# Two layers on one core: the last two weight tiles of the memory layer stay in SBUF and open its second pass

## The chip, the cores and the metric

The kernel runs on one core of one Trainium2 chip. The metric is the device time of one execution, in microseconds; the median of several executions is compared. Beside the timed executions there is one that the hardware profiler recorded. It is a separate execution with a time of its own, and all durations of single instructions come from it.

## The reference

Two layers over x of shape (2, 512, 64, 64), that is 2 images of 4096 positions with 512 channels. Both normalise their input by groups of channels and add their result to x. Layer 0 is a Mamba block (projections, a short convolution, a selective scan over 4096 positions with 1024 inner channels of 16 states); the change does not touch it. Layer 1 is a memory of 1024 rows m:

```python
def _L1_conv_ref(x, m):
    xf = jnp.transpose(x, (0, 2, 3, 1)).reshape(-1, c)   # 8192 positions x 512
    xn = _l2norm(xf)
    mn = _l2norm(m)                                      # 1024 x 512
    score = xn @ mn.T
    idx = jnp.argmax(score, axis=1)
    counts = jax.ops.segment_sum(jnp.ones(xf.shape[0], dtype=xf.dtype), idx, num_segments=k)
    esum = jax.ops.segment_sum(xf, idx, num_segments=k)
    emean = esum / (counts[:, None] + EPS_MEAN)
    new_m = m * MOVING_AVG_RATE + emean * (1.0 - MOVING_AVG_RATE)
    soft = jax.nn.softmax(score, axis=1)
    out = soft @ new_m
...
x = x + _L0_conv_ref(_gn(x), ...)
x = x + _L1_conv_ref(_gn(x), L1_conv_m)
```

new_m depends on every position, since any of them may have chosen any row. So out can't begin before all scores are known, and layer 1 has two passes.

## The kernel before

Everything is in float32. Layer 0 works in a hand-written order: its instructions go through a wrapper (line 36 in the profile) that stamps them with their place, and a table of due times sets when each step is issued. It writes x + layer 0 to DRAM as `x1d`, 256 KB at a time (tile `xo`).

Layer 1 (from line 1025) cuts the 2 x 4096 positions into 16 tiles of TT = 512, `tiles[0]` to `tiles[15]`, and each tile into SUB = 4 sub-tiles of 128 positions. P is 128, KB = 8 blocks of memory rows, CB = 4 blocks of channels. There is no order by hand here: within each engine's queue the framework's scheduler places the instructions[...]. A pool of tiles (`tc.tile_pool`) hands out `bufs` buffers for each tag, and a pool that is opened after others were closed uses their memory again; an instruction that writes into such memory waits until the last reader of what lay there is done.

*Pass 1* (loop from L1138). For each sub-tile, PE multiplies the normalised x (`xf`, loaded from `x1d` at L1060, scaled at L1062) with the normalised memory rows, which lie in `win`: the scores `pc` (L1148), 128 positions by 1024 rows. ACT copies them to `sc` (L1160) and takes the exponential `ex` (L1163), DVE scales it by the sum (L1168) and finds the largest score and its index `ix` (L1173, L1175), and `fx` is that index as a float (L1177).

Then two side branches run behind the scores:

- `match` and `add_rows` (L1098 to L1120), one sub-tile late. Positions of a sub-tile that chose the same row are added up on PE (`dg`, `pr`, `sel`, `pe`); POOL gathers the chosen rows from a table in DRAM (L1113), DVE adds, POOL scatters them back (L1120). There are two tables, `tabs[0]` and `tabs[1]`, for even and odd sub-tiles, so that a gather needn't wait for the scatter just before it.
- `exT_part` (L1088), DEFER = 6 sub-tiles late. Pass 2 needs the exponentials with the memory rows on the partitions. PE transposes 128 x 128 blocks of `ex` into `px` (L1093), four blocks to a PSUM bank, and ACT copies the bank into `exT` (L1094). A sub-tile has two such halves. When all four sub-tiles of a tile are in, ACT's queue stores `exT` (2 MB) to DRAM as `exd` (L1135). When the scores end, seven sub-tiles, 14 halves, are still to be transposed.

Between the scores of one sub-tile, `turn` (L1070) transposes the next tile's x through one PSUM bank, tag `pt`. [...]

*Pass 2* (from L1195). `new_m(kb)` loads rows kb of both tables into `e0` and `e1` (L1205, SP's queue), and DVE adds them, divides by the count, and adds the result to the decayed memory row in `win` (L1206 to L1213); `mrow` is the code's name of that part of `win`. Then PE multiplies `exT` with it: `po` (L1231), 8 products for each of the 4 channel blocks of a tile; in the trace each product is two records. Tiles go in pairs (FIRST = 2). For the first pair the blocks of memory rows are the outer loop, so that PE can start as soon as block 0 is ready:

```python
if k0 == 0:
    for kb in range(KB):
        new_m(kb)
        for j in range(len(some)):
            for cb in range(CB):
                mm(j, cb, kb)
```

For each tile SP loads `exT` from `exd` (L1223) and `xt` from `x1d` (L1225), DVE adds `po` to `xt` (L1248), and SP stores it to the output (L1249, 1 MB).

The pool `p3` (xt, and exT of every second pair) exists from before pass 1. The pool `pr3` (exT of the other pairs, e0, e1, rc) is opened after pass 1's pools are closed and lies on their memory. Pass 1's own exT buffers, two, are in `p2`.

Of the kernel before, what the change touches and what calls it, by code (L numbers as in the profile page):

```python
# [8 lines left out]
F32 = mybir.dt.float32  # L9
# [9 lines left out]
P = 128  # L19
# [30 lines left out]
def kernel(  # L50
# [17 lines left out]
    nc = tc.nc  # L68
    B, C, L = x.shape
# [6 lines left out]
    KB = K // P  # L76
# [6 lines left out]
    TT = 512  # L83
    NT = L // TT
    SUB = TT // P
# [48 lines left out]
    ROW = C + 16  # L134
# [5 lines left out]
    ov = out.rearrange("b (cb p) t -> b p cb t", p=P)  # L140
# [45 lines left out]
    with ExitStack() as l0:  # L186
        nc = InOrder(tc, tc.nc)
# [837 lines left out]
    nc = tc.nc  # L1025
    exd = [[dram.tile([P, KB, TT], F32, name=f"exd{b}_{t}") for t in range(NT)] for b in range(B)]
    p3 = ctx.enter_context(tc.tile_pool(name="q3", bufs=2))
    DEFER = 6
    KH = K // TT
    KBH = KB // KH  # L1030
    tiles = [(b, t) for b in range(B) for t in range(NT)]
# [11 lines left out]
    with ExitStack() as s:  # L1043
        p1 = s.enter_context(tc.tile_pool(name="p1", bufs=1))
        p2 = s.enter_context(tc.tile_pool(name="p2", bufs=2))
        p_ex = s.enter_context(tc.tile_pool(name="p_ex", bufs=DEFER + 1))
        ps_t = s.enter_context(tc.tile_pool(name="ps_t", bufs=1, space=PSUM))
        ps_s = s.enter_context(tc.tile_pool(name="ps_s", bufs=2, space=PSUM))
        ps_x = s.enter_context(tc.tile_pool(name="ps_x", bufs=1, space=PSUM))
# [6 lines left out]
        def load_xf(k):  # L1056

            b, t = tiles[k]
            xf = p2.tile([P, CB, TT], F32, tag="xf", name="xf")
            nc.sync.dma_start(xf, x1d[b][:, :, t * TT : (t + 1) * TT])  # L1060
            for cb in range(CB):
                nc.vector.tensor_scalar(  # L1062
                    xf[:, cb], xf[:, cb], gmu[1][b][:, cb : cb + 1], grs[1][b][:, cb : cb + 1],
                    ALU.subtract, ALU.mult,
                )
            xT = p2.tile([P, SUB, C], F32, tag="xT", name="xT")
            ss = p2.tile([P, SUB], F32, tag="ss", name="ss")
            return xf, xT, ss
# [16 lines left out]
            inv_norm(r, cur[2], wk)  # L1085
            return r

        def exT_part(ex, exT, i, kh):  # L1088

            px = ps_x.tile([P, KBH, P], F32, tag="px", name="px")  # L1090
            for q in range(KBH):
                kb = kh * KBH + q
                nc.tensor.transpose(px[:, q], ex[:, kb * P : (kb + 1) * P], ident)  # L1093
            nc.scalar.copy(  # L1094
                exT[:, kh * KBH : (kh + 1) * KBH, i * P : (i + 1) * P], px
            )
# [27 lines left out]
        behind = None  # L1124
        late = []

        def transpose_late(kh):
            if late:
                ex, exT, i, k = late[0]
                exT_part(ex, exT, i, kh)  # L1130
                if kh == KH - 1:
                    late.pop(0)
                    if i == SUB - 1:
                        b, t = tiles[k]
                        nc.scalar.dma_start(exd[b][t], exT)  # L1135

        for k in range(len(tiles)):
            cur, r = nxt, r_next  # L1138
            xf, xT, _ = cur
            if k + 1 < len(tiles):  # L1140
                nxt = load_xf(k + 1)
            exT = p2.tile([P, KB, TT], F32, tag="exT", name="exT")
            for i in range(SUB):
                pc = ps_s.tile([P, K], F32, tag="pc", name="pc")
                for kh in range(KH):
                    cols = slice(kh * TT, (kh + 1) * TT)
                    for cb in range(CB):
                        nc.tensor.matmul(  # L1148
                            pc[:, cols], xf[:, cb, i * P : (i + 1) * P], mn[:, cb, cols],
                            start=cb == 0, stop=cb == CB - 1,  # L1150
                        )
                    if kh == KH - 1 and behind is not None:
                        sel = match(*behind)
                    if k * SUB + i + DEFER < len(tiles) * SUB:
                        transpose_late(kh)
                if behind is not None:
                    add_rows(*behind, sel)

                sc = p2.tile([P, K], F32, tag="sc", name="sc")
                nc.scalar.copy(sc, pc)  # L1160
                ex = p_ex.tile([P, K], F32, tag="ex", name="ex")
                den = p2.tile([P, 1], F32, tag="den", name="den")
                nc.scalar.activation(ex, pc, AF.Exp, scale=r[:, i : i + 1], accum_out=den)  # L1163
                end = k == len(tiles) - 1 and i == SUB - 1

                def scale():
                    nc.vector.reciprocal(den, den)  # L1167
                    nc.vector.tensor_scalar_mul(ex, ex, den)  # L1168

                if not end:  # L1170
                    scale()
                mx = p2.tile([P, 8], F32, tag="mx", name="mx")
                nc.vector.max(mx, sc)  # L1173
                ix = p2.tile([P, 8], U32, tag="ix", name="ix")
                nc.vector.max_index(ix, mx, sc)  # L1175
                fx = p2.tile([P, 1], F32, tag="fx", name="fx")
                nc.vector.tensor_copy(fx, ix[:, 0:1])  # L1177
                if end:
                    scale()
                behind = k * SUB + i, xT, i, fx, ix  # L1180
                late.append((ex, exT, i, k))
                if k + 1 < len(tiles):
                    turn(nxt, i)
            if k + 1 < len(tiles):
                r_next = lengths(nxt)
        for kh in range(2 * KH):
            transpose_late(kh % KH)
        sel = match(*behind)
        for kh in range(KH):
            transpose_late(kh)  # L1190
        add_rows(*behind, sel)
        while late:
            for kh in range(KH):
                transpose_late(kh)

    with ExitStack() as s:
        pr3 = s.enter_context(tc.tile_pool(name="r3", bufs=2))
        ps_o = s.enter_context(tc.tile_pool(name="qo", bufs=8, space=PSUM))

        def new_m(kb):  # L1200

            e = []
            for i, tab in enumerate(tabs):
                e.append(pr3.tile([P, ROW], F32, tag=f"e{i}", name=f"e{i}"))
                nc.sync.dma_start(e[i], tab[kb * P : (kb + 1) * P])  # L1205
            nc.vector.tensor_add(e[0][:, : C + 1], e[0][:, : C + 1], e[1][:, : C + 1])  # L1206
            rc = pr3.tile([P, 1], F32, tag="rc", name="rc")
            nc.vector.tensor_scalar(rc, e[0][:, C : C + 1], 1.0, 1e-6, ALU.mult, ALU.add)
            nc.vector.reciprocal(rc, rc)
            nc.vector.tensor_scalar(  # L1210
                e[0][:, :C], e[0][:, :C], rc, 1.0 - RATE, ALU.mult, ALU.mult
            )
            nc.vector.tensor_add(mrow[:, kb], mrow[:, kb], e[0][:, :C])  # L1213


        FIRST = 2
        for k0 in range(0, len(tiles), FIRST):
            some = tiles[k0 : k0 + FIRST]
            pool = (p3, pr3)[k0 // FIRST % 2]
            ld, pos = [], {}  # L1220
            for b, t in some:
                exT = pool.tile([P, KB, TT], F32, tag="exT", name="exT1")
                nc.sync.dma_start(exT, exd[b][t])  # L1223
                xt = p3.tile([P, CB, TT], F32, tag="xt", name="xt1")
                nc.sync.dma_start(xt, x1d[b][:, :, t * TT : (t + 1) * TT])  # L1225
                ld.append((exT, xt))

            def mm(j, cb, kb):
                if kb == 0:
                    pos[j, cb] = ps_o.tile([P, TT], F32, tag="po", name="po1")  # L1230
                nc.tensor.matmul(  # L1231
                    pos[j, cb], mrow[:, kb, cb * P : (cb + 1) * P], ld[j][0][:, kb],
                    start=kb == 0, stop=kb == KB - 1,
# [8 lines that stand above are left out]
            for j, (b, t) in enumerate(some):  # L1242
                xt = ld[j][1]
                for cb in range(CB):
                    if k0 > 0:
                        for kb in range(KB):
                            mm(j, cb, kb)
                    nc.vector.tensor_add(xt[:, cb], xt[:, cb], pos.pop((j, cb)))  # L1248
                nc.sync.dma_start(ov[b, :, :, t * TT : (t + 1) * TT], xt)  # L1249


# [43 lines left out]
```

## Time and profile before

| | us |
|---|---|
| three timed runs | 5016.26, 5016.58, 5024.3; median 5016.58 |
| the profiled execution, its own time | 5005.66 |
| its span, first to last instruction | 5003.9 |
| layer 0 ends, first product of pass 1 | 3935.2 |
| last product of pass 1's scores done | about 4520.5 |
| last copy into exT done | 4542.5 |
| first product of pass 2 | 4555.41 |
| last add of pass 2 done | 4998.8 |

The mean granted clock of TensorE over the span is 0.968 of full speed.

Busy time, share of the span and number of instructions of each engine, from the page:

```profile
PE 4509.2 (90%) x22640; PEld 3483.1 (70%) x22640; DVE 4011.0 (80%) x3340; ACT 3529.2 (71%) x8885; POOL 3873.3 (77%) x2890
```

Layer 0 takes almost four fifths of the time, and most of the busy time of DVE, ACT and POOL is there. Layer 1 is PE's: of the 1068.7 us from 3935.2 on, 585 are pass 1 and 443 are the products of pass 2. Its two largest groups are these (busy us, mean ns of one | idle time just before them and what ended it):

```profile
L1231 PE MATMUL po<-exT,win 128*128 128x512 f32 x1024 | 442.7, 595 | 13.5 <-DVE win L1213 13.5
L1148 PE MATMUL pc<-win,xf 128*128 128x512 f32 x960 | 433.8, 592 | 0.0
```

Matmuls overlap, so the mean of one (595 ns) is more than its share of the time (0.43 us). In such rows the idle time is the engine's, and the name behind the arrow is the instruction that ended it.

The transfers of layer 1, with their size and the median from issue to landing:

```profile
exd<-exT ACTq DMA_DIRECT2D x16, 2048.0 KB, 6.3
exT<-exd SPq DMA_DIRECT2D x16, 2048.0 KB, 9.5
```

A row load e<-tab is 264 KB and lands after 2.9 us in the median (2.5 to 5.2), a load of xt or xf is 1 MB (5.8 to 6.0 us), a store of a tile's output 1 MB (10.7 us in the median where it shares the engines with a load).

### The profile page before, as it was taken

The page shows a single profiled execution, that of the slowest core. Times are in us where ns is not written, and L with a number is a line of the kernel's source. Part 1 is how long each engine was busy: PE and PEld are TensorE (multiplying, and loading weights), DVE is VectorE, ACT ScalarE, POOL GpSimd, SP SyncE. Part 2 cuts the span into 40 slices and gives each one's busy share as a digit, 9 for nine tenths or more (in the row PEclk, how much of TensorE's full clock was granted, in tenths as well). Part 3 has the DMA queues.
Part 4 walks back from the last instruction along what each step waited for, and adds up shares of the span by engine and source line. Part 5 has one row for each costly group of instructions (what it writes and reads, how often), then busy time and mean ns, then how long its engine had stood idle before and what let it go on. Part 6 is the DMA issues. An engine that isn't in the chain of part 4 may idle for free. (4 is left out here: it accounts for less than half of the span.)

```text
span 5003.9 us, 64865 instructions
## 1 busy us (share of the span) xinstructions
PE 4509.2 (90%) x22640; PEld 3483.1 (70%) x22640; DVE 4011.0 (80%) x3340; ACT 3529.2 (71%) x8885; POOL 3873.3 (77%) x2890
## 2 busy tenths in 40 slices
PE   6989889888889898998898989998886899998999
PEld 5777777777777777777777777777775555553444
DVE  5799999999999999999999999999998755553100
ACT  3788888888888888888888888888886455441000
POOL 4899999999999999999999999999999322220000
PEclk8999999999999999999999999999997899998999
DMA  5132122122222222222211212111212344334452
GB/s 214 46 108 64 64 68 67 68 67 68 71 68 68 68 68 68 75 81 77 76 64 64 66 66 70 64 64 64 66 60 106 111 162 149 137 135 165 159 164 84
DMA packets 175551, 447.72 MB, mean 89 GB/s; under 512 B 23384, under 2 KB 77784, under 8 KB 171000
## 3 DMA queue, kind: packets, MB, share of 16 engines
q1 hardware_dynamic: 162680, 375.41, 22.5%
q0 software_dynamic: 10240, 34.61, 2.2%
q10 hardware_dynamic: 2304, 33.56, 1.6%
q8 instruction: 179, 2.93, 0.2%
q14 instruction: 148, 1.21, 0.1%
HBM read 351.63 MB, written 91.88 MB: 89 GB/s over the span
## 5 line engine op out<-in xcount | busy, mean ns | idle before, releaser
L36 POOL TENSOR_TENSOR bu<-B,du 128x1020 f32<-128x1020 f32 (+1 forms) x1152 | 2453.5, 2146 | 29.0 <-DVE dA L36 15.6
L36 ACT ACTIVATE dA<-delta,A 128x256 f32<-128x256 f32 x4096 | 1957.6, 478 | 151.3 <-DVE hc L36 37.8
L36 DVE TENSOR_TENSOR_SCAN dA<-dA,bu 128x1024 f32<-128x1024 f32 x832 | 1904.3, 2289 | 61.9 <-ACT dA L36 57.0
L36 PE MATMUL yT<-ident,hc 128*128 128x128 f32 x8192 | 1095.9, 283 | 215.6 <-DVE hc L36 144.3
L36 PEld LDWEIGHTS yT<-ident,hc 128*128 128x128 f32 x8192 | 965.3, 145 | 326.9 <-DVE hc L36 198.8
L36 DVE TENSOR_TENSOR hc<-dA,C 128x1024 f32<-128x1024 f32 x832 | 1019.3, 1225 | 126.0 <-PE yT L36 40.7
L36 PE MATMUL pz<-x,win 128*128 128x256 f32 x4096 | 940.7, 383 | 15.7 <-POOL x L36 14.9
L36 PEld LDWEIGHTS pz<-x,win 128*128 128x128 f32 x4096 | 767.0, 192 | 117.2 <-POOL x L36 18.7
L36 PE MATMUL cv<-xi,cd 128*128 128x256 f32 x2048 | 468.9, 381 | 27.0 <-POOL xi L36 24.5
L36 PE MATMUL po<-z,wo 128*128 128x256 f32 x2048 | 477.2, 387 | 0.8 <-DVE z L36 0.8
L36 DVE TENSOR_TENSOR_SCAN h<-dA,bu 128x1024 f32<-128x1024 f32 x192 | 438.2, 2282 | 43.2 <-POOL hc L36 34.3
L1231 PE MATMUL po<-exT,win 128*128 128x512 f32 x1024 | 442.7, 595 | 13.5 <-DVE win L1213 13.5
L36 POOL TENSOR_TENSOR hc<-h,C 128x1024 f32<-128x1024 f32 x192 | 454.5, 2367 | 0.0
L36 PEld LDWEIGHTS cv<-xi,cd 128*128 128x128 f32 x2048 | 380.2, 191 | 84.6 <-POOL xi L36 31.2
L1148 PE MATMUL pc<-win,xf 128*128 128x512 f32 x960 | 433.8, 592 | 0.0
L36 PEld LDWEIGHTS po<-z,wo 128*128 128x128 f32 x2048 | 390.3, 195 | 54.5 <-DVE z L36 1.0
L1231 PEld LDWEIGHTS po<-exT,win 128*128 128x128 f32 x1024 | 195.6, 191 | 260.2 <-issue 260.0
L1248 DVE TENSOR_TENSOR xt<-xt,po 128x512 f32<-128x512 f32 x64 | 44.0, 689 | 375.2 <-PE po L1231 360.9
L36 ACT COPY carry<-dA 128x4 f32<-128x4 f32 x780 | 125.7, 161 | 310.5 <-DVE hc L36 304.7
L1148 PEld LDWEIGHTS pc<-win,xf 128*128 128x128 f32 x960 | 173.5, 190 | 175.9 <-issue 175.9
L1120 POOL DMA_INDIRECT tab<-rows,ix x64 | 63.2, 987 | 294.4 <-DVE den L1167 274.8
L36 PE MATMUL py<-ident,ys 128*128 128x128 f32 x512 | 84.7, 290 | 165.2 <-DVE q L36 100.2
(171 smaller groups left out, 5057.9 us busy)
## 6 DMA issues: line engine op xcount, KB each, us to landing
B<-bcd SPq DMA_DIRECT2D x128, 512.0 KB, 3.9
C<-bcd SPq DMA_DIRECT2D x128, 512.0 KB, 4.7
wo<-in_out_wT_dram SPq DMA_DIRECT2D x128, 512.0 KB, 5.2
exd<-exT ACTq DMA_DIRECT2D x16, 2048.0 KB, 6.3
exT<-exd SPq DMA_DIRECT2D x16, 2048.0 KB, 9.5
xl<-in_x_dram SPq DMA_DIRECT2D x32, 512.0 KB, 10.7
x<-in_x_dram SPq DMA_DIRECT2D x32, 512.0 KB, 3.7
xo<-in_x_dram SPq DMA_DIRECT2D x64, 256.0 KB, 4.9
```

The source lines that it names most:

```text
L36: ins = call(*args, **kwargs)
L1120: nc.gpsimd.indirect_dma_start(tab, at, rows, None)
L1148: nc.tensor.matmul(pc[:, cols], xf[:, cb, i * P : (i + 1) * P], mn[:, cb, cols], start=cb == 0, stop=cb == CB - 1,)
L1231: nc.tensor.matmul(pos[j, cb], mrow[:, kb, cb * P : (cb + 1) * P], ld[j][0][:, kb], start=kb == 0, stop=kb == KB - 1,)
L1248: nc.vector.tensor_add(xt[:, cb], xt[:, cb], pos.pop((j, cb)))
```

## The change

Four edits, all in layer 1:

- Pass 1's exT buffers move from `p2` to `p3` and are remembered in `kept`. The last FIRST = 2 tiles are not stored to `exd`. Pass 2's order becomes tiles 14, 15, 0, 1, ..., 13, and its first pair uses the kept buffers instead of loading them.
- The table rows e0 and e1 get buffers in `p3`, which no tile of pass 1 uses.
- In the last 14 halves, the transposes use `px` and the bank of `pt` in turn.
- The last tile's output is stored in four pieces of 256 KB, each after its own add.

```diff
+    kept = {}
+    FIRST = 2
...
-        def exT_part(ex, exT, i, kh):
+        def exT_part(ex, exT, i, kh, alt=False):
 
-            px = ps_x.tile([P, KBH, P], F32, tag="px", name="px")
+            if alt:
+                px = ps_t.tile([P, C], F32, tag="pt", name="px2")
+                px = px.rearrange("p (q k) -> p q k", k=P)
+            else:
+                px = ps_x.tile([P, KBH, P], F32, tag="px", name="px")
...
-        def transpose_late(kh):
+        def transpose_late(kh, alt=False):
             if late:
                 ex, exT, i, k = late[0]
-                exT_part(ex, exT, i, kh)
+                exT_part(ex, exT, i, kh, alt)
                 if kh == KH - 1:
                     late.pop(0)
-                    if i == SUB - 1:
+                    if i == SUB - 1 and k < len(tiles) - FIRST:
                         b, t = tiles[k]
                         nc.scalar.dma_start(exd[b][t], exT)
...
-            exT = p2.tile([P, KB, TT], F32, tag="exT", name="exT")
+            exT = p3.tile([P, KB, TT], F32, tag="exT", name="exT")
+            kept[tiles[k]] = exT
...
         for kh in range(2 * KH):
-            transpose_late(kh % KH)
+            transpose_late(kh % KH, kh % 2 == 1)
         sel = match(*behind)
         for kh in range(KH):
-            transpose_late(kh)
+            transpose_late(kh, kh % 2 == 1)
         add_rows(*behind, sel)
         while late:
             for kh in range(KH):
-                transpose_late(kh)
+                transpose_late(kh, kh % 2 == 1)
...
-                e.append(pr3.tile([P, ROW], F32, tag=f"e{i}", name=f"e{i}"))
+                e.append(p3.tile([P, ROW], F32, tag=f"e{i}", name=f"e{i}"))
...
-        FIRST = 2
-        for k0 in range(0, len(tiles), FIRST):
-            some = tiles[k0 : k0 + FIRST]
+        order = tiles[-FIRST:] + tiles[:-FIRST]
+        for k0 in range(0, len(order), FIRST):
+            some = order[k0 : k0 + FIRST]
...
-                exT = pool.tile([P, KB, TT], F32, tag="exT", name="exT1")
-                nc.sync.dma_start(exT, exd[b][t])
+                if k0 == 0:
+                    exT = kept[b, t]
+                else:
+                    exT = pool.tile([P, KB, TT], F32, tag="exT", name="exT1")
+                    nc.sync.dma_start(exT, exd[b][t])
...
-                nc.sync.dma_start(ov[b, :, :, t * TT : (t + 1) * TT], xt)
+                    if k0 + j == len(order) - 1:
+                        nc.sync.dma_start(ov[b, :, cb, t * TT : (t + 1) * TT], xt[:, cb])
+                if k0 + j < len(order) - 1:
+                    nc.sync.dma_start(ov[b, :, :, t * TT : (t + 1) * TT], xt)
```

## The prediction

> **What bounds the kernel now.** I read the chain of waits first, in order of time, to see which engine sets the end of each stage of layer 1, then the waits of PE and of SP's queue, then the timeline around the seam of the two passes. Columns of the chain: start, length, what.
>
> ```profile
> 4538.98 1.13 PE px L1093 x4
> 4540.77 1.13 PE px L1093 x4
> 4542.54 6.26 DMA exd<-exT
> 4549.57 3.05 DMA e<-tab
> 4555.41 442.70 PE po L1231 x1024
> ```
>
> Ahead of these lines the chain is PE's products of pass 1 (pc, L1148); behind them are 442.7 us of pass 2 without a gap. So both passes are bound by PE, and only the seam is not: last transposes, then the store of the last exT, then the load of table rows, then the first product of pass 2. PE's own waits from 3935 to 4556 (waited for: total, times, longest) agree:
>
> ```profile
> PE po L1231 <- DVE win L1213: 13.5, 1, 13.5
> PE px L1093 <- ACT exT L1094: 8.1, 12, 1.1
> PE gs_pm L36 <- DVE gs_w L36: 1.1, 1, 1.1
> ```
>
> 13.5 us idle before pass 2, 8.1 us in the last transposes, nothing else. What holds the table rows is in SP's waits:
>
> ```profile
> SPq L1205 <- DMA tab<-rows,ix: 83.2, 1, 83.2
> SPq L1205 <- DMA exd<-exT: 11.9, 1, 11.9
> ```
>
> SP waited for the last scatter into the table until about 4536.8 (the last load of pass 1 was issued at 4453.6, plus 83.2), and then 11.9 us more for the store of tile 15's exT, because the row buffers lie on memory that the store still reads. First row load: 4549.19. And the scatter itself was late (timeline):
>
> ```profile
> 4529.81 0.33 ACTq L1135 DMA_DIRECT2D exd<-exT  x1
> 4529.83 0.42 PEld L1093 LDWEIGHTS px<-ident,ex 128*128 128x128 f32 x4 [0.91 <-ACT exT L1094]
> 4529.83 0.65 PE L1093 MATMUL px<-ident,ex 128*128 128x128 f32 x4 [0.68 <-ACT exT L1094]
> 4529.90 0.98 POOL L1120 DMA_INDIRECT tab<-rows,ix  x1 [3.60 <-DVE rows L1119]
> ```
>
> It was issued together with the 2 MB store of tile 14's exT; in half-microsecond windows the DMA engines then run at up to 524 GB/s until 4536.5. The scatter before it (POOL, 4523.66) had the engines to itself: its traffic, 253 and 287 GB/s, lies in 4525.0 to 4526.0, ending 1.4 us after POOL was done with it.
>
> **The change, part by part.**
>
> *No store of tiles 14 and 15, row buffers of their own.* Both holds go. Chain of the last sub-tile, from the rows above: its gather, pe, and the DVE adds are not touched (the built order moves dg behind two more exT copies, to about 4525.3 from 4524.87, but the gather is what ends last before the add, at 4528.87). POOL issues the last scatter at 4529.90 to 4530.88, traffic ends 1.4 us later, 4532.3, seen by SP at about 4532.7 (bounds 4532.3 and 4534.0). The rows of table 0, whose last scatter was done by 4527, are in by then: in the built order SP issues both loads of table 0 first, then both of table 1. So one load decides, issued at 4532.8. The page gives 2.9 us median from issue to landing (2.5 to 5.2); before, the first add began 3.75 us after the first of four loads. I take 3.2: add at 4536.0 (bounds 4535.0 and 4538.2). DVE then interleaves two row blocks in the built order; ahead of the end of the first lie two adds 0.70, two rc 0.15, two reciprocals 0.16, one scaling 0.49 and one add into win 0.69, with eight steps of some 0.04 between: 3.5 us where one block alone took 2.35. With 0.15 us to PE (win done 4555.26, product 4555.41): first product 4539.7 instead of 4555.41, **15.7 us earlier** (bounds 13.5 and 16.7).
>
> *Two banks for the last transposes.* The 14 halves run in lock step, 0.66 PE and 0.59 ACT:
>
> ```profile
> 4531.16 0.66 PE L1093 MATMUL px<-ident,ex 128*128 128x128 f32 x4 [0.68 <-ACT exT L1094]
> 4531.86 0.59 ACT L1094 COPY exT<-px 128x512 f32<-128x512 f32 x1 [0.74 <-PE px L1093]
> ```
>
> 1.33 us a half, later 1.79 at half clock. With two banks the same 1.33 us loop serves two halves: 0.67 us each. 14 x 0.67 + 0.3 for dg from 4522.54 ends at 4532.2 instead of 4542.5. That is 7 us ahead of the tables, so this edit alone is hidden; its worth is that it isn't next: without it the first product would be at 4542.6, 2.9 us later than forecast.
>
> *The clock.* Granted clock in stretches of the seam (length, busy us of each engine, then PEclk, DMA share, GB/s):
>
> ```profile
> 4542.00:4555.00 13.00, 0.00 (x0) 0.00 (x0) 1.93 (x5) 0.51 (x1) 0.00 (x0) 0.50 0.76 282
> 4558.00:4561.00 3.00, 3.00 (x5) 1.35 (x4) 0.00 (x0) 0.00 (x0) 0.00 (x0) 0.50 0.93 363
> 4561.00:4564.00 3.00, 3.00 (x7) 1.14 (x6) 1.66 (x5) 0.00 (x0) 0.00 (x0) 0.93 1.08 440
> ```
>
> Pass 2 starts at half clock and is free of it at 4561.5: 6.1 us, half lost, 3.0 us. The new gap (4532.2 to 4539.7, 7.5 us) is longer than the 3.6 us after the last product of the kernel at which the clock fell (4998.1 to about 5001.7), so I expect a cold start again. Here a rule stands against the row: the Trainium skill, "TensorE: Matmul & The Clock Gate", part 1, says that about 3.4 us of sustained work release the clock, which by estimate would cost 1.7 us. The row says 6.1. By the row the cold start cancels (3.0 before and after); by the rule 1.3 us more is gained. I take the row, and ±1.5 us in the range.
>
> *Row loads behind tile 0's exT.* SP's queue now holds, behind the first four row loads, the 2 MB load of tile 0, which waits for memory of pass 1 (last transposes, copies and scatters, all by about 4533), and behind it the rows of blocks 2 to 7. PE needs block 2 after 16 products of 0.858 us (two records each) plus 3.0 cold: 4556.4. Blocks 2 and 3 wait for the buffers of 0 and 1 (4539.6 to 4540.4), land some 3 to 5 us later and take 2.35 us on DVE: 4548. Eight us to spare; before, the same queue had the same two 2 MB loads among the rows and PE never stopped. Cost nothing.
>
> *The start of pass 1.* The first loads of tiles 0 and 1 leave SP's queue (its two waits for exd, 60.4 us, had cost nothing: PE never waited for xf). SP now issues xf of tiles 1 and 2 ahead of the second xt. In the built order DVE scales all four blocks of tile 1's xf ahead of fx, and three of tile 2's ahead of sel; behind fx stand dg, pr and all of PE. Before, the ex scaling ended at 3948.57 and PE got px at 3948.72; now four scalings of 0.48 us put the last xf block at 3950.6, where PE, having only px and one product before the turn, would come at 3949.8. I take **1.0 us** lost, bounds 0 and 2 (the second if xf lands no earlier than its 3949.1). No gain is put down here, as PE had only 0.15 us idle.
>
> *The last store in pieces.* Before: last add done at 4998.82, issue 4998.84, traffic 4999.75 to 5002.35 at about 410 GB/s, end of span 5003.9. The like store at 4916.44 was landed when the next load went out, 4920.45: 4.0 us, of which 2.6 is traffic. A last piece of a quarter has 0.65 us of traffic; the other three lie under the 20 us of products before it. By the rows 4.0 - 1.95 = 2.05 us. A rule speaks against it: the Trainium skill, "DMA: Bandwidth & Descriptors" (sections on the anatomy of a DMA and on bandwidth), puts some 2.0 us of fixed cost[...] and advises at least 1 MiB; by estimate the last piece is then 2.65 us and saves 1.4. The 264 KB row loads' minimum of 2.5 us leans that way. I take **1.8 us saved** (1.3 to 2.1).
>
> *The rest.* The order of tiles in pass 2, exT's double buffer (two, as before), the wait of tile 2's load for a kept buffer (the same wait stood before tile 4's: SP L1223 for po, 35.4 us at the longest, unharmful): nothing.
>
> **Sum.** -15.7 + 1.0 - 1.8 = -16.5 us. The profiled execution took 5005.66 us (span 5003.9), so 4989.2 for its like. The three timed runs have the median 5016.58, 10.9 us above it; I carry the difference over: **5000.1 us**.
>
> **Rivals.**
>
> 1. *The forecast*, 0.68. Own range: gain 12.3 to 20, 4996 to 5005.
> 2. *The transposes stay the last thing.* PE's tail does not speed up (the half clock came at 4534 in the middle of it, and a colder PE gives 1.1 us for four transposes). First product 4542.6: gain 13.6, 5003.0 us. Against it: PE has twice the density there now. 0.12.
> 3. *Most of the gain is lost again at the seam*: a row load of 5.2 us in place of 3.2 (2.0 lost), as it shares the engines with the 2 MB load, and a warm-up 15 us longer than before (half of it, 7.5, lost): gain 7.0, 5009.6. For it: before, a row load among 2 MB loads took 5.2 us. Against: only table 1's first load matters, and it is issued ahead. 0.10.
> 4. *Slower:* tile 0's load holds SP's queue. It decides from about 4551 on, when block 2's rows (5.4 us to win) would miss 4556.4; each us later is a us of idle PE. Against the forecast's gain of 16.5 it would have to be held to 4567.5; held to 4573 it gives 5022. For it: it waits for a dozen semaphores, and the queue is in order. Against it: its like was issued at 4550.98 before, 1.8 us after the first row load. 0.08, with 0.02 more for what I don't see.
>
> Within 0.2% is within 10 us, which is about what a measurement of this kernel can tell from no change. Forecast and rival 2 are faster (0.80, less 0.05 for runs that scatter by the 8 us between the three shown); rival 3 is the same; rival 4 slower. So 0.75, 0.15, 0.10. Range: forecast and rival 2 with some us for the scatter of the median, 4991 to 5009.
>
> **What would show it.** Right: PE's wait for win at the start of pass 2 near 7.5 us, the first product near 16 us earlier, no exd store in the last 30 us of pass 1, px halves 0.67 us apart, the first row load of table 1 within 3 us of the last scatter, a last store of 256 KB. Wrong: PE idle inside the first 64 products (rival 4), a wait for exT's copies at their head (rival 2), PEclk at 0.5 far into pass 2 (rival 3), more than 2 us of PE waits from 3945 to 3960.

## The result

The changed kernel takes 4998.6 us in the median of seven runs (4995.48 to 5004.98), the kernel before 5017.89 us (5014.9 to 5024.3). The ratio is 0.9961, with a 95% interval of 0.9951 to 0.9971: 19.3 us, or 0.39%, faster, and by the interval between 14.6 and 24.6 us. The forecast was 5000.1 us and a gain of 16.5, which the timing alone can't tell from 19.3.

The profiled execution of the changed kernel took 4997.4 us (span 4995.7), only 8.3 us less than that of the kernel before. The reason is in layer 0, which has the same instructions in both: it ended at 3935.2 us in the one profile and at 3944.8 in the other. So I compare stages of layer 1, not spans. The cuts are the first product of pass 1, the start of the last copy of the scores (`sc`, of the last sub-tile), the first product of pass 2, and the end of its last product. All in us; each entry is rounded on its own, so a row can miss its sum by 0.1:

| profile | layer 0 ends | pass 1 | seam | pass 2 | rest | layer 1 |
|---|---|---|---|---|---|---|
| before | 3935.2 | 585.3 | 34.9 | 442.7 | 5.8 | 1068.6 |
| after | 3944.8 | 587.1 | 17.7 | 442.3 | 3.9 | 1050.9 |
| forecast for after | - | 586.3 | 19.2 | 442.7 | 4.0 | 1052.2 |

On the page, busy time and the large transfers of the changed kernel:

```profile
PE 4499.5 (90%) x22640; PEld 3475.6 (70%) x22640; DVE 4012.0 (80%) x3340; ACT 3528.1 (71%) x8885; POOL 3886.3 (78%) x2890
...
exd<-exT ACTq DMA_DIRECT2D x14, 2048.0 KB, 6.3
exT<-exd SPq DMA_DIRECT2D x14, 2048.0 KB, 9.0
```

The counts of instructions are those of before, and two stores and two loads of 2 MB are gone. PE's busy time is 9.7 us lower with the same products, 6.1 of it in layer 0, which the change leaves alone: busy time tells little of this change.

The chain of waits of the changed kernel, in order of time, at the seam (start, length, what):

```profile
4531.88 1.02 ACT sc L1167
...
4534.74 1.21 DVE ix L1182
...
4536.30 3.72 DMA rows<-tab,ix
...
4541.14 2.74 DMA tab<-rows,ix
...
4543.90 2.56 DMA e<-tab
...
4546.48 0.71 DVE e L1213
...
4548.73 0.67 DVE win L1220
...
4549.53 442.27 PE po L1241 x1024
```

Transposes and the store of exT are gone from it. What ends last is now one path through the tables: the scores of the last sub-tile, the search for the index, gather, add, scatter (2.74 us, where it took 6.9 in the profile of before), the row load, and DVE's work on it. PE's waits from the end of layer 0 to 4560 (total, times, longest):

```profile
PE po L1241 <- DVE win L1220: 6.3, 1, 6.3
PE px L1099 <- ACT exT L1100: 1.5, 5, 0.7
PE pt L1077 <- DVE xf L1064: 1.5, 1, 1.5
...
```

13.5 us before pass 2 have become 6.3, 8.1 us in the last transposes 1.5, and there is a new wait of 1.5 us at the start of pass 1. The transposes in the timeline:

```profile
4539.39 1.15 PE L1099 MATMUL px<-ident,ex 128*128 128x128 f32 x8 [0.24 <-ACT exT L1100]
4540.08 1.08 ACT L1100 COPY exT<-px 128x512 f32<-128x512 f32 x2 [0.26 <-PE px L1099]
...
4540.72 1.15 PE L1099 MATMUL px<-ident,ex 128*128 128x128 f32 x8 [0.19 <-ACT exT L1100]
```

Two halves every 1.33 us, as forecast. Their last copy ends 11.9 us after the last copy of the scores began (forecast 11.7), 5.7 us ahead of the first product.

### The profile page after: what moved, and what is told of

It is laid out like the page before. It is cut to its first block, busy times and chain, and to the rows that moved or that the text cites. A ratio compares the mean times of both kernels' runs of the same rounds, so it can differ in the third digit from the quotient of the medians.

```text
span 4995.7 us, 64857 instructions
## 1 busy us (share of the span) xinstructions
PE 4499.5 (90%) x22640; PEld 3475.6 (70%) x22640; DVE 4012.0 (80%) x3340; ACT 3528.1 (71%) x8885; POOL 3886.3 (78%) x2890
## 5 line engine op out<-in xcount | busy, mean ns | idle before, releaser
L36 PEld LDWEIGHTS pz<-x,win 128*128 128x128 f32 x4096 | 768.1, 192 | 118.3 <-POOL x L36 19.3
L1241 PE MATMUL po<-exT,win 128*128 128x512 f32 x1024 | 442.3, 595 | 6.3 <-DVE win L1220 6.3
```

The source lines that it names most:

```text
L36: ins = call(*args, **kwargs)
L1241: nc.tensor.matmul(pos[j, cb], mrow[:, kb, cb * P : (cb + 1) * P], ld[j][0][:, kb], start=kb == 0, stop=kb == KB - 1,)
```

## The experiments

Each is one profile unless it says that it was timed. The stages of all of them:

| profile | layer 0 ends | pass 1 | seam | pass 2 | rest | layer 1 |
|---|---|---|---|---|---|---|
| before_again | 3944.1 | 585.6 | 36.3 | 442.5 | 5.8 | 1070.2 |
| before_two_banks | 3949.6 | 585.7 | 25.8 | 442.3 | 5.8 | 1059.6 |
| after_one_bank | 3942.1 | 589.1 | 23.5 | 442.0 | 3.9 | 1058.5 |
| after_rows_late_pool | 3943.3 | 587.1 | 18.3 | 442.2 | 3.9 | 1051.5 |
| after_with_stores | 3949.4 | 587.1 | 24.7 | 442.4 | 3.7 | 1058.0 |
| after_xt_late | 3941.3 | 586.2 | 18.2 | 442.7 | 3.9 | 1051.0 |
| after_warm_pe | 3947.3 | 587.0 | 18.0 | 439.7 | 3.9 | 1048.6 |
| after_both | 3949.8 | 586.2 | 18.2 | 439.7 | 3.9 | 1048.0 |
| after_again_timed | 3946.4 | 586.5 | 18.3 | 441.8 | 3.9 | 1050.5 |
| after_both_timed | 3945.8 | 586.2 | 18.1 | 439.7 | 3.9 | 1048.0 |

### What of a profile repeats

The kernel before, without an edit.

> The kernel before, unchanged, profiled once more, to see what of a profile repeats. Layer 1 is cut into stages: pass 1 from the first pc product to the last copy of the scores (585.3 us before), the seam from there to the first po product (34.9), pass 2 to the last product's end (442.7), and the rest of the span (5.8). Theory: these stages repeat within 0.5 us, and the 9 us by which layer 0 ended later in the profile of the changed kernel are spread of layer 0 between executions, which has the same instructions in both: its end (3935.2 before) moves by some us here too. Rival: the change delays layer 0; then layer 0 ends at 3935 within 1 us here.

Pass 1, pass 2 and the rest repeat within 0.3 us, the seam within 1.4, which is more than I allowed. Layer 0 ended 8.9 us later than in the first profile of the same kernel, so the change doesn't delay it. Over all twelve profiles it ends between 3935.2 and 3949.8. The 1.4 us at the seam lie in the transposes: their last copy ends 22.0 us after the last copy of the scores began in the first profile and 23.4 in this one, and the first product of pass 2 follows 12.9 us later in both. What holds the rows after that is in SP's waits of this run:

```profile
SPq L1205 <- DMA tab<-rows,ix: 79.0, 1, 79.0
...
SPq L1205 <- DMA exd<-exT: 17.5, 2, 12.7
```

The wait for the last scatter ended 2.8 us after that scatter was issued (6.9 in the first profile), and the seam is no shorter for it. So in the kernel before the late scatter cost nothing; the transposes and the store behind them held the rows. A difference of less than some 1.5 us at the seam says nothing where one bank is used. The two profiles of the changed kernel differ by 0.7 us at the seam (17.7 and 18.3), 0.6 in pass 1 (587.1 and 586.5) and 0.5 in pass 2.

### Which edit earned the gain at the seam

Take each part out of the changed kernel alone. First, one bank again:

```diff
-            if alt:
+            if False:
                 px = ps_t.tile([P, C], F32, tag="pt", name="px2")
```

> The changed kernel with one bank again for the last transposes. Theory (the table rows are last at the seam, the transposes 5.7 us ahead of them): the transposes take 22.0 us from the last copy of the scores as before, the first product follows at 22.1 us, so the seam is 22.1 us against 17.65 in the changed kernel: 4.5 us lost. Rival (the two banks bring the gain at the seam): all of the 10 us that they save comes back, seam near 27.6 us.

The seam is 23.5 us: 5.8 lost (5.2 against the changed kernel's second profile), nearer to the theory's 4.5 than to the rival's 10. The chain of waits of this run ends with the transposes again:

```profile
4552.90 1.13 PE px L1099 x4
...
4554.06 0.59 ACT exT L1100
...
4554.70 441.96 PE po L1241 x1024
```

The four transposes of a half take 1.13 us here and not 0.66: they ran at half clock. In stretches of this run's tail (columns: length, busy us of PE, PEld, DVE, ACT and POOL, PEclk, DMA share, GB/s; why they are cut as they are is told below, under "The clock in the gap"):

```profile
4531.88:4535.29 3.41, 1.68 (x7) 0.61 (x7) 3.25 (x7) 2.52 (x5) 0.94 (x1) 1.00 0.00 0
4535.29:4538.71 3.42, 2.96 (x11) 2.00 (x11) 1.48 (x5) 1.47 (x3) 1.39 (x2) 0.50 0.49 147
4538.71:4542.12 3.41, 2.06 (x13) 1.29 (x12) 0.76 (x2) 1.17 (x2) 0.97 (x1) 1.00 0.48 172
4542.12:4545.53 3.41, 1.59 (x11) 0.88 (x9) 0.00 (x0) 1.60 (x3) 0.00 (x0) 1.00 0.42 136
4545.53:4548.95 3.42, 2.23 (x8) 1.43 (x8) 2.41 (x8) 1.01 (x3) 0.00 (x0) 0.50 0.98 355
```

The half clock comes and goes in the tail: seven of its fourteen halves ran slow in this run, five in the first profile of the kernel before, seven in the second. A slow half costs up to 1.79 - 1.33 = 0.46 us. The last copy into exT ends 23.4 us after the last copy of the scores began, as in before_again, and not 22.0: that is the 1.4 us beyond the theory's 22.1. Pass 1 is 2.0 us longer than the changed kernel's: 0.4 of that is a longer wait for xf at the start, and right behind that wait the clock stood at 0.50 from 3958.4 to 3961.9, with PE busy throughout, which costs half of 3.4 us.

Second, the row buffers back in the pool that lies on pass 1's memory:

```diff
-                e.append(p3.tile([P, ROW], F32, tag=f"e{i}", name=f"e{i}"))
+                e.append(pr3.tile([P, ROW], F32, tag=f"e{i}", name=f"e{i}"))
```

> The changed kernel with the table rows' buffers back in the pool that lies on pass 1's memory. Theory (with the last exT store gone, that memory is free when the last transposes and the last scatter are done, 12.0 us after the last copy of the scores, which is when the last scatter lands anyway): at most 1 us lost, as the two loads of table 0 no longer run ahead: seam 16.5 to 18.7 us against 17.65. Rival (buffers of their own are what frees the rows): seam over 20 us.

18.3 us, within the spread of the changed kernel itself (17.7 and 18.3). Buffers of their own bring nothing that shows, once the store of tile 15 is gone. Table 0's early loads let the first add begin 14.6 us after the last copy of the scores in the changed kernel, against 15.8 here; half of that is given back on DVE, which finished block 0 in 2.3 us here and works on two blocks at once there (3.05 us to the first product against 2.5). The converse, own row buffers in the kernel before, was not tried.

Third, the two stores left in, though nobody reads them:

```diff
-                    if i == SUB - 1 and k < len(tiles) - FIRST:
+                    if i == SUB - 1:
```

> The changed kernel that still stores the exT of tiles 14 and 15 (nobody reads them back). Theory (the last scatter is late behind tile 14's 2 MB store: 6.9 us from issue to landing before, 2.7 in the changed kernel): the scatter takes some 6.9 us again, seam 21.8 us against 17.65, 4.2 us lost. Rival (only the wait of the row loads for tile 15's store counted, which own buffers end): seam 17.4 to 18.2 us.

The seam is 24.7 us: 7.1 lost (6.4 against the changed kernel's second profile), where the theory had 4.2 and the rival none. The direction is the theory's, its size too small. The chain of this run:

```profile
4540.91 4.41 DMA rows<-tab,ix
...
4546.45 8.16 DMA tab<-rows,ix
...
4555.00 3.98 DMA e<-tab
```

and the two stores in its timeline:

```profile
4542.38 0.35 ACTq L1141 DMA_DIRECT2D exd<-exT  x1
...
4548.46 0.33 ACTq L1141 DMA_DIRECT2D exd<-exT  x1
```

With two banks the stores come only 6.1 us apart, one ahead of the last scatter and one right behind it, so the scatter runs beside both: 8.16 us against 2.74. The gather and the row load, 4.41 and 3.98 against 3.72 and 2.56, pay as well. No row load waits for a store's memory here, so what the stores cost is in the transfers that run beside them.

### The two banks in the kernel before

The edit of `exT_part` and `transpose_late` from the change, and nothing else of it.

> The kernel before with the two banks for the last transposes and nothing else. Theory (in the kernel before, the end of the transposes releases tile 15's store, the store the row loads, these the first product): the transposes end 12.0 us after the last copy of the scores instead of 22.0, the store of tile 15 lands some 7 to 8 us later beside the other store, rows and DVE take 6.3 us: seam 25 to 27.5 us against 34.9 and 36.3 in the two profiles of the kernel before. Rival (the scatter and not the transposes holds the rows there, so that the banks are hidden as in the forecast): seam 32 us or more.

25.8 us, 9 to 10.5 less than the two profiles of the kernel before, so the theory holds. The same edit is worth 9 to 10.5 us there and 5.2 to 5.8 us on top of the others: in the kernel before, every microsecond of the transposes stood ahead of the store, and the store ahead of the rows. The waits of SP's queue in this run:

```profile
SPq L1209 <- DMA tab<-rows,ix: 81.3, 1, 81.3
...
SPq L1209 <- DMA exd<-exT: 4.7, 1, 4.7
```

The wait for tile 15's store is 4.7 us, where it was 11.9. From 25.8 to the changed kernel's 17.7 to 18.3 the rest of the change brings 7.5 to 8.1 us.

### The start of pass 1

DVE scales tile 1's xf before PE can transpose it, and `fx` is what `dg`, and then PE, waits for. First the kernel before, then the changed kernel:

```profile
3948.49 0.15 DVE L1177 CAST fx<-ix 128x1 f32<-128x1 uint32 x1
...
3949.11 1.92 DVE L1062 TENSOR_SCALAR xf<-xf,gmu,grs 128x512 f32<-128x512 f32 x4 [0.47 <-DMA xf<-x1d]
```

```profile
3959.60 1.91 DVE L1064 TENSOR_SCALAR xf<-xf,gmu,grs 128x512 f32<-128x512 f32 x4 [1.52 <-DMA xf<-x1d]
...
3961.43 0.14 DVE L1184 CAST fx<-ix 128x1 f32<-128x1 uint32 x1
```

Counted from the first product, the scaling begins 13.9 us in before and 14.8 us in after. The next run takes the loads of xt out of SP's queue there:

```diff
-                xt = p3.tile([P, CB, TT], F32, tag="xt", name="xt1")
-                nc.sync.dma_start(xt, x1d[b][:, :, t * TT : (t + 1) * TT])
+                xt = pr3.tile([P, CB, TT], F32, tag="xt", name="xt1")
+                if k0 > 0:
+                    nc.sync.dma_start(xt, x1d[b][:, :, t * TT : (t + 1) * TT])
...
                             mm(j, cb, kb)
+                for j, (b, t) in enumerate(some):
+                    nc.sync.dma_start(ld[j][1], x1d[b][:, :, t * TT : (t + 1) * TT])
```

> The changed kernel with the loads of xt for the first pair of pass 2 moved behind the first round of products (and xt's buffers in the pool that opens with pass 2), so that nothing of pass 2 stands in SP's queue at the start of pass 1. Theory (the changed kernel loses 1.8 us of pass 1 because PE waits 1.5 us for tile 1's xf, which lands late and is asked for early): PE's wait for xf is gone and pass 1 takes 585.3 us or less against 587.1. Rival (it is the order on DVE, all of xf ahead of fx, that costs): pass 1 stays within 0.5 us of 587.1. The seam may lengthen by 0.5 us as the two xt loads now lie among the rows.

PE's wait for xf is gone, but pass 1 takes 586.2 us, so 0.9 us of the 1.8 came back: between theory and rival. In its place a wait for fx of 0.6 us appeared. This edit also changed the built order on DVE (scaling of xf ahead of the search for the index), so it can't tell the two causes apart, and how they share the loss stays open. With the second profile of the changed kernel at 586.5 the loss itself is 0.9 to 1.8 us.

### The clock in the gap

```diff
+        idle = ps_e.tile([P, C], F32, tag="pe", name="idle")
+        for n in range(6):
+            nc.tensor.matmul(idle, ident, exT[:, KB - 1], start=n == 0, stop=n == 5)
```

> The changed kernel with six products of ident with the finished exT, whose result nobody reads, between the last transpose and pass 2 (6 x 0.858 us = 5.15 us in a gap of 6.3). Theory (the clock falls because PE idles in the gap, at 4.7 us after its last work in the changed kernel's profile): the granted clock stays at 1.00 into pass 2, which takes 439.7 us instead of 442.3, with the seam as it was, 17.6 us. Rival (the half clock at the start of pass 2 has another cause than the gap): pass 2 stays at 442.3 us.

Granted clock in stretches of the gap and of the start of pass 2 (columns as above), first in the changed kernel:

```profile
4541.03:4544.44 3.41, 1.98 (x16) 1.36 (x13) 0.00 (x0) 2.28 (x5) 0.97 (x1) 1.00 0.24 95
4544.44:4547.85 3.41, 0.00 (x0) 0.00 (x0) 1.28 (x3) 0.00 (x0) 0.00 (x0) 1.00 0.78 264
4547.85:4551.27 3.42, 1.74 (x2) 0.84 (x3) 2.62 (x8) 0.00 (x0) 0.00 (x0) 0.50 0.99 378
4551.27:4554.68 3.41, 3.41 (x5) 1.35 (x4) 0.00 (x0) 0.00 (x0) 0.00 (x0) 0.50 0.94 345
4554.68:4558.09 3.41, 3.41 (x9) 1.52 (x8) 1.78 (x5) 0.00 (x0) 0.00 (x0) 1.00 1.11 462
```

then with the six products in the gap:

```profile
4546.00:4552.00 6.00, 5.42 (x12) 2.20 (x12) 2.64 (x8) 0.23 (x1) 0.00 (x0) 1.00 0.70 229
4552.00:4555.00 3.00, 2.67 (x7) 1.27 (x8) 1.27 (x3) 0.00 (x0) 0.00 (x0) 1.00 1.00 385
```

The clock stays at 1.00, and pass 2 takes 439.7 us, to the tenth what the theory said, in all three runs that have the six products. The seam stays within its spread. So the half clock comes from the gap, and costs 2.6 us in the changed kernel's first profile and 2.1 in its second.

The traces also show when the clock changes. In each of the twelve, all changes of the granted clock (87 to 95 in each) are whole multiples of 3.413 us apart, and the stretches above and in the run with one bank are cut at such steps. Around the seam of all twelve, a stretch at full clock was followed by half clock where PE had been busy for 49% of it or less (1.68 and 1.59 us of 3.41 with one bank, 0.00 here) and by full clock where it had been busy for 55% or more (1.98 here); a stretch at half clock was followed by full clock from 86% busy on (2.96 with one bank), and by half clock at 76% or less. In layer 0 the limits lie elsewhere: there the clock stayed full behind stretches with 41%. So a cold start of pass 2 lasts for the rest of the stretch in which it begins and one whole stretch more: 4.2 to 6.0 us in the nine profiles that have one. Pass 2 takes 439.7 us and half of that, to within 0.03 us in each of them, so the spread of pass 2 is this.

### Both, and timed

> The changed kernel with both of these: xt late and the six products in the gap. Theory: the two gains lie in different stages and add, layer 1 takes 1050.9 - 1.8 - 2.6 = 1046.5 us. Rival: one undoes the other at the seam (the xt loads ahead of the rows push the first product out, and the gap is longer than the six products): layer 1 at 1049 us or more.

Layer 1 takes 1048.0 us: less than the changed kernel's 1050.9, but 1.5 us more than the 1046.5 of the theory, 0.9 of it because xt brought 0.9 instead of 1.8, and 0.6 at the seam.

> The changed kernel once more, timed in five rounds on the chip on which the next one is timed. Theory: about 17 to 18 us under the kernel before (the sum of its stages in the profiles), ratio near 0.9965; stages of layer 1 as in its first profile within 0.5 us, wherever layer 0 ends. Rival (the 19 us of the first measurement hold something beside layer 1): 0.996 or less.

> The changed kernel with xt late and six products in the gap, timed in five rounds. Theory: by its stages 2.8 us under the changed kernel (layer 1 1048.1 against 1050.9), so ratio to the kernel before near 0.9960; the two intervals overlap, as 2.8 us are less than the runs scatter. Rival (what the profile shows is not there without it): no lower than the changed kernel.

On one chip, five rounds each: the changed kernel 4998.91 us, ratio 0.9962 (0.9949 to 0.9976); with both edits 4996.92 us, ratio 0.9958 (0.9944 to 0.9971); the kernel before 5018.62 us. The stages of layer 1 again differ by 2.5 us (1050.5 and 1048.0), and the medians by 2.0, but the intervals overlap. By its stages the version with both edits is the fastest of all; by its time alone that isn't shown. For the changed kernel the ratio lies between what theory and rival had, so that run doesn't decide: the stages of its two profiles against those of the two of the kernel before give 17.7 to 19.7 us, the two timings 19.3 and 19.7.

## Why the prediction was right

**The bound.** PE in both passes, one seam between them that isn't PE's: pass 2 changed by 0.4 us, pass 1 by 1.8, the seam by 17.2. Right.

**Stores gone, row buffers of their own: 15.7 us forecast as the whole of the seam's gain.** 17.2 measured. Counted from the last copy of the scores, the forecast had the last row load issued at 12.3 us, DVE's first add at 15.5, the first product at 19.2; the profile has the load at 12.0, the add at 14.6, the product at 17.7. The mis-sized terms: the row load, taken at 3.2 us, took 2.56 with only two loads side by side; DVE's interleaved block, taken at 3.5 us and 0.15, took 3.05 in all, as its short steps overlap. The reason given was half right. In the changed kernel the stores would make the gather, the last scatter and the row load late, which is worth 7.1 us by experiment. But in the kernel before the late scatter, which the prediction names as a hold of its own, was covered by the wait for the store, as before_again shows. And the row buffers' own place, named in the heading of that step beside the stores, is worth nothing that shows.

**Two banks hidden, 2.9 us if they were missing.** They are hidden: 5.7 us of slack. Without them 5.8 us are lost and not 2.9. The tables were 1.5 us faster than forecast, so the transposes would be next that much sooner, and in the run with one bank two more halves of the tail fell on the half clock than in the profile the forecast was made from, 1.4 us: 2.9 + 1.5 + 1.4. How much the banks are worth without the other edits I had not seen. Against the two profiles of the kernel before, the banks alone bring 9.1 to 10.5 us of the seam, the other edits alone 11.4 to 12.8, and all together 16.6 to 18.6, less than the two added up. The sum was right because it was made over the path, not over the edits.

**The clock.** A cold start again, as the row said, and by the row no change. It lasted 5.2 us (4549.5 to about 4554.7) against the row's 6.1 and the 3.4 us of the rule in the Trainium skill ("TensorE: Matmul & The Clock Gate", part 1); the measurement lies between them, nearer to the row. The rule's 3.4 us is one whole stretch of the 3.41 us told of above; what the estimate from it left out is the rest of the stretch in which pass 2 begins, 2.6 us in the profile of before and 1.7 in that of the changed kernel. Where in a stretch pass 2 begins differs between executions, so that the two cold starts cancel to within 0.4 us is in part luck: the nine of them cost 2.1 to 3.0 us. Priced by experiment: 2.6 us.

**Row loads behind tile 0's exT: nothing.** Right. PE's only wait in pass 2 is the one ahead of it. Rival 4 has nothing in the profile for it: the queue was held for no longer than the rows needed. Nor have rival 2, with the transposes done 5.7 us ahead, and rival 3, with a row load of 2.56 us.

**The start of pass 1: 1.0 us lost, bounds 0 and 2.** 1.8 and, in the second profile, 1.2 against the first profile of the kernel before. The order on DVE was as read, but one reason was wrong. I held that xf would come sooner with one xt load less ahead of it; it was issued 6.63 us after the last x1d store (6.96 before) and landed 7.3 us after that (6.0 before). The landing varies by itself: it took 6.5 us in the second profile of each kernel, and 7.0 in after_xt_late, where no xt load runs beside it. So the longer landing is not shown to come from the change, and the cause stays open.

**The last store: 1.8 us saved.** 1.9. The last piece landed 2.0 us after its issue. The estimate from the rows was 1.95 us, that from the fixed cost in "DMA: Bandwidth & Descriptors" 2.65, and the rows were right: most of that price was already contained in the 1.4 us which a whole store took beside its traffic. The page's 2.0 us is its fit for transfers that GpSimd issues, and this store is issued by SP.

**What I misjudged about the measure.** The forecast for the profiled execution, 4989.2 us, missed (4997.4), and not for anything in the change: one profile's span carries some 15 us of spread from layer 0. The median over runs, 5000.1 against 4998.6, came out since the difference was carried over to it. That it came so near is in part luck: the seam gained 1.5 us more than forecast and pass 2 0.4, pass 1 lost 0.8 more, and the median of the three runs that it starts from lies 1.3 us under that of seven. The stages give a gain of 17.7 us, and the forecast's 16.5, these 17.7 and the timed 19.3 all lie within the interval of the timing.

## What to carry to other kernels

At a seam between two passes, write down every path that must end before the second begins, with its length, and make the sum over the longest; what an edit is worth depends on which others are in, here 9 to 10.5 us or 5.2 to 5.8 for the same one. A large store near a small transfer that everybody waits for costs time (7.1 us here), even where nobody waits for its memory. When a seam can't be closed, keeping TensorE busy in it with work that nobody reads took away the cold start behind it, here 2.1 to 2.6 us of pass 2, with the seam unchanged.

## What was unexpected of the hardware

- A 264 KB scatter took 2.74 us from issue to landing alone and 8.16 between two 2 MB stores. Beside one it depends on when the store starts: 6.9 us where it was issued 0.1 us ahead of the scatter (before), 4.5 where 4.0 us ahead (before_two_banks), 2.8 where 1.2 us behind (before_again).
- With one bank, where PE is busy for about half of the tail, the clock dropped to half for stretches of it in all three profiles looked at (before, before_again, after_one_bank), at different places. With two banks PEclk was 1.00 from 4536 to 4543, for the same transposes. So a clock can be lost without any long gap: the longest single wait of PE in those tails was 1.1 us.
- How long after PE's last work the clock falls is not fixed: 4.7 us at the seam of the changed kernel (4543.2 to about 4547.9), 3.6 us at the end of the kernel before, 1.7 us at the seam of after_rows_late_pool. The fall itself lies on the steps of 3.413 us in all of them.
- Layer 0's end moves by 14.6 us between executions with the same instructions, while the stages of layer 1, but for the half clock in them, repeat within 0.3 to 0.7 us.
